# One planned kernel: load costs of the head, W^T a as columns, one operation for the weights' remainder, and scores spread by TensorE

## The chip, the cores and the metric

The kernel runs on one core of a Trainium2 chip. The metric is device time in microseconds, the median of several runs; lower is better. The engines are named as in the profile: PE is TensorE's matmul stream, PEld its weight loads, DVE is VectorE, ACT is ScalarE, POOL is GpSimd, and SP is SyncE, which issues nearly all DMAs.

## What is computed

Two graph layers on 64 graphs of 256 nodes with 256 features. The first is a gated graph network of three steps (matrix products, an aggregation over the adjacency, and a GRU cell), the second a graph attention layer; each has a layer norm and a relu ahead of it and adds its input.

```python
h = relu(layernorm(x))                      # x: (64, 256, 256)
for i in range(3):                          # gated network, A = (adj != 0)
    m = h @ weight[i]
    aggr = einsum('bst,bsd->btd', A, m)
    gi = aggr @ w_ih.T + b_ih;  gh = h @ w_hh.T + b_hh
    r = sigmoid(i_r + h_r);  z = sigmoid(i_z + h_z)
    n = tanh(i_n + r * h_n);  h = (1 - z) * n + z * h
x = x + h
h = relu(layernorm(x))                      # attention
v = h @ W.T
e = (v @ a_left)[:, :, None] + (v @ a_right)[:, None, :]
e = where(e > 0, e, 0.2 * e);  e = where(adj == 0, -1e9, e)
x = x + softmax(e) @ v
```

## The kernel before

The 64 graphs are worked on in 32 pairs. A pair is a stream of operations: layer norm and relu, turning h into columns, three gated layers, then the attention of each graph. The aggregation is done first on h, and `weight[i]` is folded into `w_ih` once in the head (the product called G, L643), so that a gate is two products with fixed matrices: `hh` with h and matrix `i` with the aggregate.

Every large product keeps more accuracy than one pass gives: an operand is split into a rounded top part in float32r and two float16 parts, and three passes are accumulated (L706 for gates, L845 for the aggregation, L1010 and L1029 for the attention). A weight matrix `m` is split by `factor` into `fac[m]` (the top), `low[m][:, 1]` (the remainder times 4096) and `low[m][:, 0]` (the top again in float16). In `factor` ScalarE writes the top (L592), VectorE writes the remainder into a float32 scratch tile (L594) and scales it into float16 (L597), and GpSimd casts the top (L599). The other splits of the head, for the operands of G, are in `three` (L626, L627, L629).

Nothing is issued in the order in which the code is written. Each operation is entered in a `Plan` with an engine, an occupancy and a latency in ns, and the tiles that it reads and writes. `Plan.run` then places the operations one by one: of those that are ready it takes the one that can start first, and among these the one with the lowest priority value, which is a due time less the length of the chain behind it and less a lead. The leads are a table `LEAD` of some 800 numbers by operation name, with the prefixes "first", "pen", "late" and "last" for pair 0 and the last three pairs:

```python
for o in self.order():
    d = deadline(o.pair) if o.due is None else o.due
    for s in o.succs:
        d = min(d, s.prio)
    o.prio = d - o.lat
for o in self.ops:
    o.prio -= o.lead
```

The order found is fixed when the kernel is built; on the chip each engine runs its own stream in that order and waits on semaphores. The planned times serve the order alone. Up to four pairs are in flight, and the 8 PSUM banks, 28 float32 tiles and the other tiles are handed out by the same plan.

Names that matter in what follows:

- The head (`setup`): `rows_of` loads weight matrices, two blocks of 128 rows (256 KB) with each DMA (L558); `load` brings x and adj of a graph, 256 KB each (L515); `bank_of` and `transposed` turn blocks by TensorE (L608, L569); "warm" runs eleven transposes of the identity (L530). `va` holds W^T a for both halves of a, spread over all partitions (L661, copied by L665).
- `dma_turn` turns a tile by the DMA's transposing copy (L738), gathers it (L743), and `join` puts it in place by ScalarE (L751). "back" turns h back into rows after a layer, by `dma_turn` where `away` holds, else by TensorE (L916; the last pair's halves L898).
- Attention: "dot" forms the two scores of each node on VectorE (L944). The right-hand scores must lie along the free axis on every partition: "line" and "right" send them to DRAM and back, broadcast (L953, L956), and for the last pair TensorE transposes them instead (L965). Then "leaky" (L970), "mask" (L973), "max" (L975), "exps" (L981, last pair L1055), "p turn", "mix", "project", "out" (L1045, L1082) and "store" (L1048, L1085). The last two pairs mix and project in plain float32 (L1018 and L1040; the last pair in halves, L1071 and L1079). `far` is true for all pairs but the last.

Of the kernel before, what the change touches and what calls it, by code (L numbers as in the profile page):

```python
# [10 lines left out]
F32 = mybir.dt.float32  # L11
# [19 lines left out]
    "A": -227000, "G": 61000, "b_nh": -3500, "b_rz": -2000, "back 0": -13500, "back 0 gather": -253500,  # L31
    "back 0 of 0": 23000, "back 0 of 1": -20500, "back 1": -55500, "back 1 gather": -20000, "back 1 of 0": 24500,
    "back 1 of 1": 49000, "back copy 1": -67500, "c0 0": -103000, "c0 1": 2000, "c0 d": -82000, "c1 0": -14500,
    "c1 1": 4000, "c1 d": 16000, "d add 0": 73500, "d add 0 of 0": -74000, "d add 0 of 1": -6000, "d add 1": -32000,
    "d add 1 of 0": -25000, "d add 1 of 1": 43500, "d mul 0": -71000, "d mul 0 of 0": 35000, "d mul 0 of 1": -14000,
    "d mul 1": 91500, "d mul 1 of 0": 46000, "d mul 1 of 1": 12000, "d sub 0": 40500, "d sub 0 of 0": 34000,
    "d sub 0 of 1": -11000, "d sub 1": 11500, "d sub 1 of 0": 22000, "d sub 1 of 1": 26000, "dot 0": 44000,
    "dot 1": 138000, "exps 0": -58500, "exps 0 0": -500, "exps 0 1": 5000, "exps 1": 137000, "exps 1 1": 46500,
    "fill": -2000, "first A": -116500, "first A16": 14000, "first back 1": 9500, "first c0 0": 12000,
    "first c0 1": 500, "first c1 1": 3000, "first d add 0": -25500, "first d add 1": 500, "first d mul 0": -22000,  # L40
    "first d mul 1": 78500, "first d sub 0": -8000, "first d sub 1": -48000, "first dot 0": -163000,
    "first dot 1": 1000, "first exps 0": -43500, "first exps 1": -15500, "first fill": 4000, "first g0 0": -42000,
    "first g0 1": 32000, "first g0 d": 38500, "first g1 0": -8000, "first g1 1": -79500, "first g1 d": 65000,
    "first h0 1": -15000, "first h1 0": 1000, "first h1 1": -32000, "first h1 d": -500, "first hi 0": 13500,
    "first hi 1": 40000, "first in 0 eps": -16000, "first in 0 pow": 55500, "first in 0 relu": 10000,
    "first in 0 shift": 32500, "first in 0 stats": 500, "first in 1 eps": -14500, "first in 1 relu": 40000,
    "first in 1 shift": -1000, "first in 1 stats": 20000, "first in hi 0": 20000, "first in hi 1": 174000,
    "first in lo 0": 80000, "first in lo 1": -16000, "first leaky 0": -23000, "first leaky 1": -122000,
    "first line 1": -1500, "first lo 0": -8000, "first lo 1": -18500, "first load": -23500, "first m0 0": 43500,
    "first m0 1": -112500, "first m0 d": 21500, "first m1 0": 16000, "first m1 1": 5000, "first m1 d": 3500,  # L50
    "first mask 0": -20000, "first mask 1": 3000, "first mid 0 eps": -111500, "first mid 0 pow": -5000,
    "first mid 0 shift": -500, "first mid 0 stats": 31000, "first mid 1 eps": 46500, "first mid 1 pow": -12000,
    "first mid 1 relu": 29500, "first mid 1 shift": 1000, "first mid 1 stats": -38000, "first mix 0": 46500,
    "first mix 1": -42000, "first nh 0 scale": 16000, "first nh 0 topF": 14000, "first nh 1 scale": 32000,
    "first ni 0 topF": -41500, "first ni 1 topF": 1000, "first out 0": 18000, "first out 1": -16000,
    "first p copy 0": 14000, "first p turn 0": -1000, "first p turn 0 gather": 26500, "first p turn 1 gather": -1000,
    "first p0 0": 18000, "first p0 1": -500, "first p0 d": -16000, "first p1 1": 12000, "first p1 d": -11000,
    "first project 0": -3000, "first prop 0": 500, "first r 0": -16500, "first r 0 topF": -16000,
    "first r 0 topT": -500, "first r 1": 90000, "first r 1 topF": 1000, "first r 1 topT": 92000,
    "first recip": -16000, "first res 0": -52000, "first res 1": -32500, "first right 0": 2000,  # L60
    "first right 1": -37500, "first store": 8000, "first tanh 0": 500, "first tanh 1": 1000, "first total": 2000,
    "first turn 0": 15500, "first turn 1": 54000, "first turn copy 0": 1000, "first turn copy 1": -8000,
    "first u 0": 8000, "first u 1": -12000, "first u add 0": -16000, "first u add 1": -97000, "first z 0": 26500,
# [135 lines left out]
    "va": 13000, "va copy": 40500, "vec": -51000, "w 0": 192500, "w copy": -77500, "w d": 84500, "w load": 2500,  # L199
    "w turn": 1500, "w up": 41000, "warm": -38000, "z 0": 34500, "z 0 of 0": -23500, "z 0 of 0 topF": -101500,  # L200
    "z 0 of 1": -31000, "z 0 of 1 topF": -260500, "z 0 topF": -647000, "z 1": 39000, "z 1 of 0": -24000,
    "z 1 of 0 topF": -69500, "z 1 of 1": -8000, "z 1 topF": -1212500,
}


# [920 lines left out]
```

## Time and profile before

| | |
|---|---|
| median of 3 runs | 1944.39 us (1941.63 to 1945.19) |
| the profiled execution's own time | 1944.63 us |
| its span in the profile | 1942.8 us |
| PE busy | 1928.9 us, 99% of the span |
| DVE, ACT busy | 1671.6 us and 1599.6 us |
| POOL busy | 228.0 us |
| granted TensorE clock, mean | 0.999 |

The span runs from the first to the last instruction. A busy PE need not be at its peak, since matmuls are pipelined, but consecutive starts in the timeline show its pace. Idle time of an engine is listed in front of the instruction that ended it, with the engine whose work released it. Lines such as L706 are lines of the kernel as printed above.

### The profile page before, as it was taken

The page shows a single profiled execution, that of the slowest core. Times are in us where ns is not written, and L with a number is a line of the kernel's source. Part 1 is how long each engine was busy: PE and PEld are TensorE (multiplying, and loading weights), DVE is VectorE, ACT ScalarE, POOL GpSimd, SP SyncE. Part 2 cuts the span into 40 slices and gives each one's busy share as a digit, 9 for nine tenths or more (in the row PEclk, how much of TensorE's full clock was granted, in tenths as well). Part 3 has the DMA queues.
Part 4 walks back from the last instruction along what each step waited for, and adds up shares of the span by engine and source line. Part 5 has one row for each costly group of instructions (what it writes and reads, how often), then busy time and mean ns, then how long its engine had stood idle before and what let it go on. Part 6 is the DMA issues. An engine that isn't in the chain of part 4 may idle for free.

```text
span 1942.8 us, 31802 instructions
## 1 busy us (share of the span) xinstructions
PE 1928.9 (99%) x10312; PEld 1223.1 (63%) x10312; DVE 1671.6 (86%) x3964; ACT 1599.6 (82%) x2799; POOL 228.0 (12%) x280
## 2 busy tenths in 40 slices
PE   8999999999999999999999999999999999999998
PEld 6656666666665666666666656666666666566677
DVE  7678889888889888898888898888988888988877
ACT  6668888888988888888889888888888888888876
POOL 4001011111011111011110111110111111110100
PEclk9999999999999999999999999999999999999999
DMA  4137676667767667866678776677765667666732
GB/s 142 33 77 147 131 144 119 119 123 139 147 117 130 120 133 131 156 110 125 119 141 138 136 120 120 124 136 153 114 130 118 139 131 146 116 125 117 125 69 72
DMA packets 734471, 239.45 MB, mean 123 GB/s; under 512 B 658256, under 2 KB 734304, under 8 KB 734304
## 3 DMA queue, kind: packets, MB, share of 16 engines
q1 hardware_dynamic: 734272, 237.41, 64.8%
q8 instruction: 81, 1.33, 0.3%
q14 instruction: 86, 0.70, 0.1%
q10 hardware_dynamic: 32, 0.01, 0.0%
HBM read 61.09 MB, written 16.84 MB: 40 GB/s over the span
## 4 chain that ended last, share of the span: by engine, by line
PE 93%; ACT 2%; DMA 2%; DVE 1%; SPq 1%; issue 0%; POOL 0%; ACTq 0%; DVEq 0%
PE bank L706 75%; PE bank L845 9%; PE bank L1029 4%; PE bank L1010 4%; DMA full<-full 2%; PE bank L643 0%; ACT full L751 0%; ACT round L674 0%; DMA full<-in_L_gnn_w_ih_dram 0%; PE bank L1018 0%; DVE half L676 0%; ACT full L874 0%; SPq L743 0%; ACT half L679 0%; PE bank L1040 0%
## 5 line engine op out<-in xcount | busy, mean ns | idle before, releaser
L706 PE MATMUL bank<-half,low_hh 128*128 128x512 f16 (+1 forms) x2352 | 613.2, 375 | 0.8 <-DVE half L676 0.8
L706 PE MATMUL bank<-half,low 128*128 128x512 f16 (+1 forms) x2352 | 612.9, 376 | 0.3 <-ACT half L679 0.2
L706 PE MATMUL bank<-round,fac_hh 128*128 128x512 f32 (+1 forms) x1176 | 433.2, 455 | 0.0
L706 PEld LDWEIGHTS <-low 128*128 128x128 f16 x2352 | 209.5, 98 | 270.9 <-issue 68.8
L706 PEld LDWEIGHTS <-low_hh 128*128 128x128 f16 x2352 | 215.4, 98 | 254.7 <-issue 47.1
L706 PE MATMUL bank<-round,fac 128*128 128x512 f32 (+1 forms) x1176 | 372.8, 411 | 0.0
L751 ACT COPY full<-full 128x1024 uint16<-128x1024 uint16 x304 | 351.8, 1174 | 20.5 <-DMA full<-full 19.6
L773 POOL TENSOR_TENSOR small<-small,nhalf 128x2 f32<-128x2 f32 x128 | 126.2, 994 | 1403.4 <-DVE small L771 1380.7
L676 DVE SCALAR_TENSOR_TENSOR half<-bank,round 128x512 f16<-128x512 f32 (+1 forms) x254 | 173.2, 684 | 107.2 <-ACT round L674 76.7
L706 PEld LDWEIGHTS bank<-round,fac_hh 128*128 128x128 f32 x1176 | 218.3, 189 | 69.0
L706 PEld LDWEIGHTS bank<-round,fac 128*128 128x128 f32 x1176 | 218.7, 188 | 57.7 <-ACT round L674 0.2
L874 ACT ACTIVATE full<-full,vec 128x512 f32<-128x512 f32 (+1 forms) x196 | 139.4, 711 | 84.7 <-DVE full L872 82.8
L676 DVE SCALAR_TENSOR_TENSOR half<-full,round 128x512 f16<-128x512 f32 (+1 forms) x254 | 170.1, 680 | 28.0 <-ACT round L674 27.4
L679 ACT ACTIVATE half<-bank 128x512 f16<-128x512 f32 (+1 forms) x254 | 154.0, 607 | 31.6 <-PE bank L1010 19.4
L674 ACT ACTIVATE round<-full 128x512 fp32r<-128x512 f32 (+1 forms) x254 | 157.5, 637 | 27.0 <-DVE full L885 26.9
L877 ACT ACTIVATE full<-bank,b_rz 128x512 f32<-128x512 f32 (+1 forms) x196 | 132.3, 675 | 48.7 <-PE bank L706 46.1
L728 ACT ACTIVATE bank<-bank,b_nh 128x512 f32<-128x512 f32 (+1 forms) x196 | 126.5, 646 | 53.8 <-PE bank L706 53.2
L864 ACT ACTIVATE full<-bank,b_rz 128x512 f32<-128x512 f32 (+1 forms) x196 | 135.1, 690 | 24.9 <-PE bank L706 24.6
L881 DVE TENSOR_TENSOR full<-full,full 128x512 f32<-128x512 f32 (+1 forms) x196 | 142.5, 727 | 12.1 <-ACT full L874 11.2
L869 DVE SCALAR_TENSOR_TENSOR full<-full,bank 128x512 f32<-128x512 f32 (+1 forms) x196 | 131.1, 670 | 18.4 <-ACT full L864 14.7
L674 ACT ACTIVATE round<-bank 128x512 fp32r<-128x512 f32 (+1 forms) x254 | 145.9, 605 | 1.2 <-PE bank L845 1.1
L682 DVE TENSOR_SCALAR half<-full 128x512 f16<-128x512 f32 (+1 forms) x254 | 124.6, 500 | 19.9 <-ACT full L751 19.8
(119 smaller groups left out, 2564.5 us busy)
## 6 DMA issues: line engine op xcount, KB each, us to landing
full<-full SPq DMA_DIRECT2D x484, 128.0 KB, 3.9
x<-in_x_dram SPq DMA_DIRECT2D x64, 256.0 KB, 3.2
adj<-in_adj_dram SPq DMA_DIRECT2D x64, 256.0 KB, 3.2
full<-in_x_dram SPq DMA_DIRECT2D x64, 256.0 KB, 3.3
full<-full SPq DMA_DIRECT2D x248, 64.0 KB, 2.2
out_dram<-full SPq DMA_DIRECT2D x62, 256.0 KB, 3.5
full<-line SPq DMA_DIRECT2D x62, 128.0 KB, 3.9
full<-full SPq DMA_TRANSPOSE x304, 3.2
```

The source lines that it names most:

```text
L674: act(f"{name} 0{of}", cut(A512 if bank else C512), lambda: nc.scalar.activation(v0.t[:, cols], v.t[:, cols], AF.Copy, scale=up), r=[(v, h ...
L676: dve_(f"{name} 1{of}", cut(V512), lambda: nc.vector.scalar_tensor_tensor(v1.t[:, cols], v.t[:, cols], up, v0.t[:, cols].bitcast(F32), op0 ...
L679: act(f"{name} d{of}", cut(A512), lambda: nc.scalar.activation(vd.t[:, cols], v.t[:, cols], AF.Copy, scale=up * unit), r=[(v, has)], w=[(v ...
L706: return [(j, lambda start, j=j, kb=kb: nc.tensor.matmul(bank.t[:, cols], fs(j, kb), s[kb][j].t[:, cols], start=start, stop=True, skip_gro ...
L728: act(name + " scale", fit(575, part), lambda: nc.scalar.activation(bank.t[:, cols], bank.t[:, cols], AF.Identity, bias=bias), r=[("b_nh", ...
L751: act(name, 1065, lambda: nc.scalar.copy(dst.t.bitcast(U16).rearrange("p (j n b) -> p j n b", j=2, b=2), src.t.bitcast(U16).rearrange(f"p ...
L845: nc.tensor.matmul(pa.t[:, ts(g, N)], b, m[:, ts(sb, N)], start=(n == 0), stop=True, skip_group_check=True)
L864: act(f"r {db}{of}", fit(575, part), lambda b=r_, k=pr, db=db, cols=cols: nc.scalar.activation(b.t[:, cols], k.t[:, cols], AF.Tanh, bias=b ...
L869: dve(f"u {db}{of}", fit(S512, part), lambda u=u, k=ph, b=r_, cols=cols: nc.vector.scalar_tensor_tensor(u.t[:, cols], b.t[:, cols], 1.0, k ...
L874: act(f"tanh {db}{of}", fit(615, part), lambda u=u, en=en, cols=cols: nc.scalar.activation(u.t[:, cols], u.t[:, cols], AF.Tanh, bias=b_i[: ...
L877: act(f"z {db}{of}", fit(575, part), lambda b=z_, k=pz, db=db, cols=cols: nc.scalar.activation(b.t[:, cols], k.t[:, cols], AF.Tanh, bias=b ...
L881: dve2(f"d sub {db}{of}", fit(V512, part), lambda u=u, d=d, cols=cols: nc.vector.tensor_sub(d.t[:, cols], d.t[:, cols], u.t[:, cols]), r=[ ...
```

## The change

In words:

- `dma_first`: loads of x, adj and the residual's x of pair 0 are planned with 1000 ns of SP and a latency of 3900 ns; `rows_of` charges 1000 ns where it charged 500. Head operations have names per matrix ("w load ih", "w 1 f0"), so that the lead table can treat them apart, and the whole table has new values (three of some 800 entries are as they were).
- `factor`: where the scale times 4096 is 1, the remainder is written at once as source minus 4096 times the top. With the new scales this holds for the twelve splits of G and for two of `w_hh` (its second half). GpSimd's cast has a region of its own, and gates and "project" name it as read.
- `va`: TensorE forms W^T a as four columns with W as the stationary operand, VectorE copies them, and four transposes of broadcast columns spread them.
- `away`: the third layer's "back" of pair 0 goes by DMA, as in later pairs.
- "dot": for the last pair the right-hand scores of both blocks come first, then the left-hand ones.
- "right": the last pair but one also spreads its right-hand scores by TensorE.

The lead table's rows for the head, old and new, with the other rows left out:

```diff
-    "va": 13000, "va copy": 40500, "vec": -51000, "w 0": 192500, "w copy": -77500, "w d": 84500, "w load": 2500,
-    "w turn": 1500, "w up": 41000, "warm": -38000, "z 0": 34500, "z 0 of 0": -23500, "z 0 of 0 topF": -101500,
...
+    "w 1 0": -227000, "w 1 1": 15000, "w 1 2": -44000, "w 1 f0": 1000, "w 1 f2": 9500, "w 1 fW": 38000,
...
+    "w load 0": 143000, "w load 1": 85500, "w load 2": -31500, "w load W": 37000, "w load full": 5000,
+    "w load hh": -8000, "w load ih": 192500, "w load x": 79000, "w turn": -151500, "w turn 2": -21500,
```

The code:

```diff
+    def dma_first(name, kb, fn, **kw):
+        plan.op(name, "SP", 1000, 3900, fn, **kw)
...
-        dma("load", 256, lambda: nc.sync.dma_start(parts(b), rows(src, g)), w=[(b, ALL)], ahead=ahead, **kw)
+        (dma if g >= G else dma_first)("load" if g >= G else f"w load {cls}", 256, lambda: nc.sync.dma_start(parts(b), rows(src, g)), w=[(b, ALL)], ahead=ahead, **kw)
...
-                plan.op("w load", "SP", 500, 3900, lambda b=b, r0=r0: nc.sync.dma_start(parts(b), view[:, r0 : r0 + 2, :]), w=[(b, ONE)])
+                plan.op(f"w load {tag}", "SP", 1000, 3900, lambda b=b, r0=r0: nc.sync.dma_start(parts(b), view[:, r0 : r0 + 2, :]), w=[(b, ONE)])
...
-            dve_("w 1", 75 + 1.04 * n, lambda: nc.vector.scalar_tensor_tensor(
-                t.t[:, :n], src(), up, top.bitcast(F32), op0=ALU.mult, op1=ALU.subtract),
-                r=[(b, ONE), (f"fac{m}", (key + (0,),))], w=[(t, ONE)])
-            dve2("w up", 75 + 0.52 * n, lambda: nc.vector.tensor_scalar(cross, t.t[:, :n], SPLIT, None, op0=ALU.mult),
-                 r=[(t, ONE)], w=[(f"fac{m}", (key + (1,),))])
-            pool("w d", 90 + 1.1 * n, lambda: nc.gpsimd.tensor_copy(rem, top.bitcast(F32)),
-                 r=[(f"fac{m}", (key + (0,),))], w=[(f"fac{m}", (key + (1,),))])
+            if up * SPLIT == 1.0:
+                dve_(f"w 1 f{m}", 75 + 1.04 * n, lambda: nc.vector.scalar_tensor_tensor(
+                    cross, top.bitcast(F32), -SPLIT, src(), op0=ALU.mult, op1=ALU.add),
+                    r=[(b, ONE), (f"fac{m}", (key + (0,),))], w=[(f"fac{m}", (key + (1,),))])
+            else:
...
+            pool(f"w d f{m}", 90 + 1.1 * n, lambda: nc.gpsimd.tensor_copy(rem, top.bitcast(F32)),
+                 r=[(f"fac{m}", (key + (0,),))], w=[(f"fac{m}", (key + (2,),))])
...
-        transposed(lambda c: whhT[c].t[:, :H], lambda c: (whhT[c], ONE), whh_n[3:], 2 * D - H, up=UP_F)
+        transposed(lambda c: whhT[c].t[:, :H], lambda c: (whhT[c], ONE), whh_n[3:], 2 * D - H, up=UP_G)
...
-            factor("hh", whhT[kb], kb, 1, bank=False)
+            factor("hh", whhT[kb], kb, 1, bank=False, up=C)
...
-                    factor(i, pg, db, half, up=1.0 / UP_H)
+                    factor(i, pg, db, half, up=C)
...
-        pl = Buf("bank")
-
-        def go():
+        pc, pl = Buf("bank"), Buf("bank")
+
+        def columns_of():
+            for db in range(DB):
+                for ob in range(DB):
+                    nc.tensor.matmul(pc.t[:, 2 * db : 2 * db + 2], parts(Wb)[:, ob, ts(db, P)], vec[:, ob : 2 * DB : DB],
+                                     start=(ob == 0), stop=(ob == DB - 1))
+
+        def spread():
             for n in range(2):
-                for ob in range(DB):
-                    c = n * DB + ob
-                    nc.tensor.matmul(pl.t[:, ts(n, D)], vec[:, c : c + 1].to_broadcast([P, P]), parts(Wb)[:, ob, :],
-                                     start=(ob == 0), stop=(ob == DB - 1))
-
-        pe("va", 4 * MM, go, r=[(Wb, ONE), ("vec", ONE)], w=[(pl, ONE)])
+                for db in range(DB):
+                    nc.tensor.transpose(pl.t[:, n * D + db * P : n * D + (db + 1) * P],
+                                        va_c[:, 2 * db + n : 2 * db + n + 1].to_broadcast([P, P]), ident)
+
+        pe("va", 4 * 110, columns_of, r=[(Wb, ONE), ("vec", ONE)], w=[(pc, ONE)])
+        dve("va column", 70, lambda: nc.vector.tensor_copy(va_c, pc.t[:, : 2 * DB]), r=[(pc, ONE)], w=[("va_c", ONE)])
+        pe("va spread", 4 * TR, spread, r=[("va_c", ONE), ("ident", ONE)], w=[(pl, ONE)])
...
-                               (f"fac{m}", tuple((kb, half, j) for kb in range(DB) for j in range(2))) for m, _ in ts_], w=[(bank, ONE)]))
+                               (f"fac{m}", tuple((kb, half, j) for kb in range(DB) for j in range(3))) for m, _ in ts_], w=[(bank, ONE)]))
...
-            away = far and p > 0
+            away = far and (p > 0 or i > 1)
...
-            for nb in range(NB):
-                for n in range(2):
+            for nb, n in [(nb, n) for nb in range(NB) for n in range(2)] if far else [(nb, n) for n in (1, 0) for nb in range(NB)]:
...
-                        r=[(hb[g], (nb,)), ("va", ONE)], w=[(sm, (c,)), (sc[g], (nb,))])
+                        r=[(hb[g], (nb,)), ("va", ONE)] + ([] if far or n == 1 else [(sm, (14, 15))]), w=[(sm, (c,)), (sc[g], (nb,))])
...
-            if p < NPAIR - 1:
+            if p < NPAIR - 2:
                 line, pR = Buf("line"), Buf("full")
```

## The prediction

> **What bounds the kernel now.** I read in this order: the page's busy table, the table of stretches, what TensorE waited for, the timeline of the head and of the tail, the chain of waits at both ends, and the queue rows.
>
> First the page's busy table, then the stretches (columns: stretch, its length, busy time of PE, PEld, DVE, ACT, POOL with counts, granted clock, DMA share, GB/s).
>
> ```profile
> PE 1928.9 (99%) x10312; PEld 1223.1 (63%) x10312; DVE 1671.6 (86%) x3964; ACT 1599.6 (82%) x2799; POOL 228.0 (12%) x280
> ```
>
> ```profile
> 0.00:10.00 10.00, 6.65 (x29) 5.62 (x29) 4.45 (x21) 3.68 (x7) 4.88 (x14) 1.00 0.80 257
> 10.00:20.00 10.00, 8.96 (x57) 6.24 (x55) 8.14 (x20) 9.18 (x25) 4.27 (x9) 1.00 0.60 182
> 20.00:30.00 10.00, 9.73 (x61) 7.24 (x61) 9.70 (x26) 9.04 (x23) 5.79 (x10) 1.00 0.12 37
> 30.00:40.00 10.00, 9.20 (x49) 5.45 (x48) 9.73 (x27) 5.19 (x11) 3.03 (x6) 1.00 0.52 114
> ...
> 1000.00:1200.00 200.00, 199.97 (x1051) 124.51 (x1050) 177.97 (x426) 166.37 (x286) 24.60 (x28) 1.00 0.73 126
> ...
> 1920.00:1943.00 23.00, 17.07 (x90) 13.91 (x88) 11.28 (x38) 9.45 (x25) 0.69 (x1) 0.91 0.15 49
> ```
>
> TensorE bounds it: 1928.9 of 1942.8 us, and 199.97 of 200 in the body. It idles 13.9 us in all: 5.5 in the first 40 us (40 less 34.54), 5.7 from 1920 on, 2.7 between. A schedule can win these, a slowed clock, and whatever TensorE work is deleted. Everything else is cover.
>
> Next, the timeline of TensorE in the head (start, length, instruction, idle before it and its releaser).
>
> ```profile
> 3.27 0.98 SPq L558 DMA_DIRECT2D full<-in_L_gnn_w_hh_dram  x2
> ...
> 5.32 0.54 SPq L558 DMA_DIRECT2D full<-in_L_gnn_w_ih_dram  x1
> ...
> 6.90 3.46 PE L608 MATMUL bank<-ident,full 128*128 128x128 f32 x15 [0.42 <-DMA full<-in_L_gnn_w_ih_dram]
> ...
> 11.24 0.77 PE L608 MATMUL bank<-ident,full 128*128 128x128 f32 x5 [0.88 <-DMA full<-in_L_gnn_w_ih_dram]
> ...
> 13.71 0.60 PE L643 MATMUL bank<-round,round 128*128 128x384 f32 x2
> ```
>
> The third w_ih load is issued at 5.32, behind x, weight 0, w_hh and adj, and lands at 11.2; the first product G (L643) starts only at 13.71. The third thing is the tail.
>
> ```profile
> 1904.22 0.95 ACT L970 ACTIVATE full<-full,small 128x256 f32<-128x256 f32 x2
> ...
> 1911.04 0.95 ACT L970 ACTIVATE full<-full,small 128x256 f32<-128x256 f32 x2
> ...
> 1918.37 2.00 PE L1018 MATMUL bank<-full,full 128*128 128x256 f32 x8 [0.64 <-ACT full L751]
> ...
> 1925.23 3.68 PE L1018 MATMUL bank<-full,full 128*128 128x256 f32 x8 [1.98 <-ACT full L751]
> ```
>
> L970 is the leaky step of the last pair but one, L1018 its two mix products. TensorE's last gate product starts at 1917.35; then it waits for the other pair's attention (0.64 and 1.98 us), and the second mix takes 3.68 us where the first took 2.00.
>
> **The change part by part.**
>
> *Order of the loads.* The planner charges a head load 1000 ns of its queue in place of 500 or 600, and the leads are per matrix. By the lead table (a larger lead goes earlier; the loads' own chains differ by some 10 us only, the leads by 40 and more) SP issues w_ih x3, weight 0, then weight 1 and x, and w_hh and weight 2 late. Between 2 and 12 us the stretches show 294, 277, 332, 368 and 360 GB/s, mean 326, so 262 KB take 0.80 us. With the first load landed at 3.5 (as now), the third w_ih lands at 5.1, not 11.2, and weight 0 at 5.9. The Trainium skill, DMA: Bandwidth & Descriptors, section "Anatomy of one DMA", fits 2.0 us + bytes/436 GB/s for a transfer issued by GpSimd: an estimate of 2.6 us for this size, whatever is ahead. By that the third w_ih would land at 7.9 now; the new order moves its issue from 5.32 to about 1.7 (0.74 and two issues of 0.47), so it would win 3.6 us on that load. The row says 5.9 us now from issue to landing and 6.1 us won. I use the row. ScalarE then needs four L626 of 0.47 and L629 (0.96 and 0.76 for pairs): from about 4.5, two and two for the first half of w_ih (1.9 us) and 1.7 for weight 0, so G could start at 8.1. Until then TensorE has 0.25 + 16 transposes of 0.115, so of the 4.1 us after the warm-up (ends 3.97) it idles 2.0, as much as it does now before 8.1 (0.42 + 1.14 + 0.42). What goes is the idle after 8.1: 0.88, about 0.2 around 13, 0.17 and 0.80, so -2.0. Ends: 0 if ScalarE (9.18 and 9.04 of 10) takes over as the limit, -4.0 if all idle after 4 goes.
>
> *Remainder of the weights in one operation.* Fourteen L597 (12 of 0.352, two near 0.4) leave VectorE: 5.0 us of the 27.6 it works from 10 to 40. The 0.55 us operation stays. This is cover for the line above (the 0.80 at 34.32 waits for VectorE), not a second gain. GpSimd's cast (0.51) now has its own key, and gates wait for it; it lies 10 us ahead of them, so 0.
>
> *W^T a as columns.* Eight L661 matmuls take 1.73 us in the chain. The new eight move two columns; no row shows that. The nearest has 128 columns: L1071, 16 in 1.78, 0.11 each, so 0.89; the lower end is the planner's 0.44. I take 0.89. The four spreading transposes: 0.11 each by L815 (8 in 0.87), 0.44. Net -0.4 (to -0.85). One small VectorE copy more (0.17 by L547); TensorE has other work between.
>
> *Back of pair 0, third layer, by DMA.* Eight L916 transposes leave TensorE, 0.11 each: -0.9, in a stretch that is 50.00 of 50 busy. In their place SP issues two transposes (1.3 each) and four gathers (0.65 each), ScalarE makes two copies of 1.16, and VectorE reads SBUF; the result comes some 8 us later (3.2 to land, 3.9 for the gather, 1.16). Pair 1's gates cover it; without that cover TensorE would stand for the difference, once. Behind these SP issues stand pair 2's loads, which have a pair's time, so 0 (upper end +0.5).
>
> *Right-hand scores of the last pair but one on TensorE.* Two DMAs per graph go (L953, L956, 3.2 and 3.9 us to land, and SP holds the second until 1905.78); four transposes come, +0.44. The dots end at 1894.8 and 1900.9, the leaky steps start 9.4 and 10.1 us later; with 0.7 for transposes and the wait they start some 9 us earlier. From leaky to mix it is 14.2 us in both graphs, so the mixes could start at about 1910 and 1916, inside the gates. A PSUM bank is held meanwhile.
>
> That does not give 9 us, because the work only changes places. Two mix and two project calls are 6.9 us at 1.73 (8 in the chain's rows). What ends the kernel then is the last pair's own path from the last gate: 25.2 us now. Without the other pair in between it would be 17.4: 7.3 to the dots (0.5 to the tanh, 0.9 for two updates, 0.5 back, 0.75 residual, 1.9 norm, 1.3 relu, the rest dots), 10.1 from there (right 0.3, leaky 0.9, mask 0.75, max 0.7, exps, turn, copy, mix, project and out 4.8, store 2.7). With all four calls ahead of the last gate, gates end at 1917.6 + 7.3 and the kernel at 1942.3: -0.5. With none ahead and none waited for, it is 20.0 (25.2 less waits of 0.64, 0.24, 1.98 and 0.30, 1.7 of a slowed clock, shown below, and 0.3 of the dots): 1918.0 + 20.0 = 1938.0, -4.8. With two ahead, 1921.5 + 18.7 (midway) = 1940.2, -2.6. The lead table does not tell which; I take the middle, -2.6.
>
> Here a rule weighs. The Trainium skill, TensorE: Matmul & The Clock Gate, section on the HAM clock gate, has the clock halve after an idle window of about 3.4 us. This trace is harsher: the wait was 1.98 us and the granted clock went to 0.64, 0.50, 0.50, 0.66 between 1925 and 1929, which cost 3.68 - 2.00 = 1.7 us. By the rule a wait that short is worth itself, by the row nearly twice that; the -2.6 leans on the row. The rule also warns of the head, should the longer gap before G cool the clock; with 0.47 busy of 2 us between 4 and 6 the trace still shows 1.00, so I put 0.
>
> *Dots of the last pair, right-hand ones first.* The spread starts two dots (0.7 us) earlier, beside the left dots; 0.3 of it lies on the path and is inside the -2.6.
>
> *All leads redrawn.* 0, from +2 to -1.5: TensorE waits 2.7 us between 40 and 1900.
>
> Sum: -2.0 - 0.4 - 0.9 - 2.6 = -5.9, against the profiled execution's 1944.63 (span 1942.80 and 1.83 around it), so 1938.7. That execution lies 0.24 above the median of the runs shown, 1944.39, so I say 1938.5.
>
> **The rivals.** *The idle only moves.* ScalarE, 91% busy from 10 to 30, holds G back as the DMA did, and the other pair's products all go ahead of the last gates. What stays is the deleted work: -0.4 - 0.9 - 0.5 = -1.8, 1942.6. For it: both engines above 90% there. Against it: 5.0 us less VectorE work, and ScalarE's idle 4.2 us at the start. Here belongs also that the change does not do what it says: orders come from planned times, and if the late mixes stay where they are, the tail gives nothing.
>
> *The body breaks.* The only one on the other side. Engines run fixed orders, and 300 leads of the repeating pair are redrawn for one plan. If one VectorE or ScalarE step lands in the wrong place, TensorE waits in each of about 30 pairs. VectorE has 11% slack (177.97 of 200), and L676 already waits 104 us for L674. At 0.20 us a pair it eats the 5.9; from 0.33 the kernel is slower by over 0.2%; at 0.5 it costs 15 us, 1953.5. Against it: 199.97 of 200 shows that such an order can be planned.
>
> *All idle goes.* Head -4.0, tail -4.8, columns -0.85, back -0.9: -10.6, 1934.
>
> **How the numbers follow.** The main case 0.52, all idle 0.12, moved idle 0.23, body 0.13. A measurement of this kernel tells about 0.2%, 3.9 us, from no change: the runs shown span 1941.6 to 1945.2. Main and best case lie beyond that on the faster side (0.64); the moved idle is inside, with 0.02 of the body (0.25); slower 0.11. The range 1934.0 to 1944.5 holds the first three with their bounds and leaves out the broken body. The likeliest case alone: 1935.5 to 1940.5.
>
> **What would show it.** w_ih issued three in a row and G's first matmul near 8 us; no L597 for fac 0 to 2; TensorE's idle in 0 to 40 near 3.5; VectorE below 9 in 20 to 40; eight fewer L916; the other pair's leaky near 1896; no clock below 1.00 after 1920. I am wrong if G starts after 12, if the clock drops in the head, if TensorE is under 199 of 200 in the body, or if the path from the last gate is still 25 us.

## The result, and the profile after

The changed kernel takes 1939.36 us (median of nine runs, 1935.76 to 1941.12) against 1944.3 for the kernel before in the same session: a ratio of 0.9975, 95% interval 0.9964 to 0.9985, or 4.9 us less. Its profiled execution took 1937.42 us with a span of 1935.6, 7.2 us less than the profiled execution before. Single executions of either kernel lie up to 4 us from their median, so the two profiles show where time went, and the medians how much.

The page's busy table:

```profile
PE 1927.1 (100%) x10312; PEld 1215.8 (63%) x10312; DVE 1647.4 (85%) x3951; ACT 1600.9 (83%) x2801; POOL 195.7 (10%) x280
```

PE busy falls by only 1.8 us, so most of the gain is idle time and slowed clock that went. The table of stretches (stretch, length, busy time of PE, PEld, DVE, ACT, POOL, granted clock, DMA share, GB/s):

```profile
0.00:10.00 10.00, 7.56 (x32) 6.14 (x33) 3.64 (x15) 5.46 (x12) 3.50 (x12) 1.00 0.78 244
10.00:20.00 10.00, 10.00 (x57) 7.25 (x57) 7.41 (x23) 8.48 (x20) 5.07 (x9) 1.00 0.74 230
20.00:30.00 10.00, 10.00 (x70) 7.54 (x69) 9.09 (x29) 8.06 (x22) 3.84 (x7) 1.00 0.01 2
30.00:40.00 10.00, 10.00 (x51) 5.93 (x49) 7.99 (x19) 7.16 (x16) 5.96 (x12) 1.00 0.55 128
1000.00:1200.00 200.00, 200.00 (x1047) 123.77 (x1045) 173.68 (x425) 167.27 (x286) 19.46 (x26) 1.00 0.72 125
1760.00:1830.00 70.00, 68.64 (x372) 42.94 (x371) 59.92 (x139) 58.64 (x99) 5.31 (x8) 1.00 0.73 122
1920.00:1935.60 15.60, 11.07 (x68) 8.97 (x66) 6.84 (x23) 6.66 (x20) 0.00 (x0) 1.00 0.20 68
```

All of the idle in the first 40 us now lies in the first ten (2.44 us; it was 5.45 over the four rows). The body stays full. One stretch is worse than before: 1.36 us of idle between 1760 and 1830, where before had none from 1700 to 1860. The timeline of the head, SP and then TensorE (start, length, instruction, idle before it and its releaser):

```profile
0.74 1.47 SPq L570 DMA_DIRECT2D full<-in_L_gnn_w_ih_dram  x3
2.25 0.47 SPq L570 DMA_DIRECT2D full<-in_L_gnn_weight_dram  x1
```

```profile
3.76 1.65 PE L626 MATMUL bank<-ident,full 128*128 128x128 f32 x6
...
6.42 2.18 PE L626 MATMUL bank<-ident,full 128*128 128x128 f32 x9 [0.39 <-DMA full<-in_L_gnn_w_ih_dram]
9.29 1.12 PE L626 MATMUL bank<-ident,full 128*128 128x128 f32 x4 [0.69 <-DMA full<-in_L_gnn_weight_dram]
10.06 0.99 PE L661 MATMUL bank<-round,round 128*128 128x384 f32 x2
10.86 2.78 PE L661 MATMUL bank<-half,half 128*128 128x384 f16 x8
```

The third load of w_ih releases TensorE at 6.42, where before it did so at 11.2. (The wait at 9.29 is for weight 1, whose turn stands ahead of G; it was issued at 3.79 and took 5.5 us.) G starts at 10.06, 3.65 us earlier than before and straight behind that turn. The timeline of ScalarE, which splits the turned blocks, shows what G would have to wait for next:

```profile
4.80 0.49 ACT L644 ACTIVATE round<-bank 128x384 fp32r<-128x384 f32 x1 [1.55 <-PE bank L626]
...
8.17 1.25 ACT L647 ACTIVATE half<-bank 128x384 f16<-128x384 f32 x3
9.28 0.69 ACT L644 ACTIVATE round<-bank 128x256 fp32r<-128x256 f32 x2
```

The top parts of weight 0 (128x256, L644) come behind all eight pieces of w_ih (128x384) and end at 9.97. G's first product needs the first of them, done at 9.70, and starts at 10.06, so ScalarE stands close behind weight 1's turn as a limit. The eight float16 products of G take 2.78 us, where before they took 1.47; more on that below. The end, ScalarE's leaky steps and then TensorE from the last gate product:

```profile
1896.46 0.84 ACT L994 ACTIVATE full<-bank,small 128x256 f32<-128x256 f32 x2 [0.40 <-PE bank L989]
...
1900.26 0.83 ACT L994 ACTIVATE full<-bank,small 128x256 f32<-128x256 f32 x2
```

```profile
1913.54 0.40 PE L731 MATMUL bank<-round,fac 128*128 128x256 f32 x2
1913.78 1.89 PE L1042 MATMUL bank<-full,full 128*128 128x256 f32 x8
...
1916.54 1.99 PE L1042 MATMUL bank<-full,full 128*128 128x256 f32 x8
1918.37 3.62 PE L1064 MATMUL bank<-wT,full 128*128 128x256 f32 x16
...
1927.68 0.93 PE L1087 MATMUL bank<-ident,full 128*128 128x128 f32 x4 [0.94 <-ACT full L1079]
```

The other pair's leaky steps (L994) come 7.8 and 10.8 us earlier than before. All four of its mix and project calls (L1042, L1064) stand behind the last gate product and start without a wait: they fill the time in which the last pair's residual, norm and dots run. The waits of 0.64 and 1.98 us and the slowed clock between them are gone. What is left is 0.94 us, behind the last pair's own exps (L1079), and 0.32 us.

To place the gain, I give each matmul of both traces its usual pace (the median distance to the next start for its shape and operands). What a stretch has beyond the sum of these is lost time: idle, a slow clock, or a matmul record missing from the trace.

| lost, us | before | after | difference |
|---|---|---|---|
| 0 to 40 | 9.03 | 7.16 | -1.9 |
| 40 to 200 | 1.21 | 0.52 | -0.7 |
| 200 to 1700 | 5.51 | 4.83 | -0.7 |
| 1700 to 1860 | 0.34 | 2.19 | +1.9 |
| 1860 to the last gate | 2.03 | 0.47 | -1.6 |
| start of the last gate product to the end (whole path) | 25.31 | 21.97 | -3.3 |
| TensorE work deleted ahead of the last gate | | | -0.8 |

They sum to -7.2 (rounded), the difference of the two spans. Against the medians' -4.9, 2.3 us of this belongs to the two executions. The rows themselves vary: in `after_again`, a second execution of the changed kernel (below), the first 40 us lose 2.0 us less than in the table, but 40 to 200 loses 0.9 more and 1700 to 1860 1.0 more, and its span is only 0.3 us shorter.

### The profile page after: what moved, and what is told of

It is laid out like the page before. It is cut to its first block, busy times and chain, and to the rows that moved or that the text cites. A ratio compares the mean times of both kernels' runs of the same rounds, so it can differ in the third digit from the quotient of the medians.

```text
span 1935.6 us, 31604 instructions
## 1 busy us (share of the span) xinstructions
PE 1927.1 (100%) x10312; PEld 1215.8 (63%) x10312; DVE 1647.4 (85%) x3951; ACT 1600.9 (83%) x2801; POOL 195.7 (10%) x280
## 4 chain that ended last, share of the span: by engine, by line
PE 95%; DMA 1%; ACT 1%; DVE 1%; SPq 1%; issue 0%; ACTq 0%
PE bank L731 76%; PE bank L870 9%; PE bank L1053 4%; PE bank L1034 4%; DMA full<-full 1%; PE bank L661 1%; SPq L768 0%; DMA full<-in_L_gnn_weight_dram 0%; ACT full L804 0%; ACT round L717 0%; PE bank L1095 0%; PE bank L1042 0%; ACT full L776 0%; DVE half L701 0%; PE bank L626 0%
## 5 line engine op out<-in xcount | busy, mean ns | idle before, releaser
L731 PE MATMUL bank<-half,low_hh 128*128 128x512 f16 (+1 forms) x2352 | 613.7, 376 | 0.0
L731 PE MATMUL bank<-half,low 128*128 128x512 f16 (+1 forms) x2352 | 611.7, 375 | 0.1
L731 PE MATMUL bank<-round,fac_hh 128*128 128x512 f32 (+1 forms) x1176 | 411.6, 437 | 0.0
L731 PE MATMUL bank<-round,fac 128*128 128x512 f32 (+1 forms) x1176 | 394.9, 425 | 0.0
L731 PEld LDWEIGHTS <-low 128*128 128x128 f16 x2352 | 216.2, 98 | 267.3 <-issue 45.4
L731 PEld LDWEIGHTS <-low_hh 128*128 128x128 f16 x2352 | 206.2, 98 | 265.3 <-issue 78.8
L731 PEld LDWEIGHTS bank<-round,fac 128*128 128x128 f32 x1176 | 218.6, 189 | 61.4
L731 PEld LDWEIGHTS bank<-round,fac_hh 128*128 128x128 f32 x1176 | 217.2, 189 | 62.7
L798 POOL TENSOR_TENSOR small<-small,nhalf 128x2 f32<-128x2 f32 x128 | 113.3, 893 | 1266.7 <-DVE small L796 1197.6
L701 DVE SCALAR_TENSOR_TENSOR half<-bank,round 128x512 f16<-128x512 f32 (+1 forms) x254 | 171.6, 683 | 50.2 <-ACT half L704 31.8
L701 DVE SCALAR_TENSOR_TENSOR half<-full,round 128x512 f16<-128x512 f32 (+1 forms) x254 | 170.3, 679 | 8.9 <-ACT round L699 6.2
L699 ACT ACTIVATE round<-bank 128x512 fp32r<-128x512 f32 (+1 forms) x254 | 152.0, 599 | 16.6 <-PE bank L870 11.5
L718 DVE SCALAR_TENSOR_TENSOR half<-full,round 128x512 f16<-128x512 f32 x184 | 125.9, 686 | 41.4 <-ACT round L717 35.6
L908 DVE SCALAR_TENSOR_TENSOR full<-full,full 128x512 f32<-128x512 f32 (+1 forms) x196 | 130.4, 676 | 33.4 <-ACT full L902 33.1
L906 DVE TENSOR_TENSOR full<-full,full 128x512 f32<-128x512 f32 (+1 forms) x196 | 132.8, 678 | 23.3 <-ACT full L899 23.0
L704 ACT ACTIVATE half<-bank 128x512 f16<-128x512 f32 (+1 forms) x254 | 142.6, 601 | 3.7 <-PE bank L870 3.1
```

Source lines behind the costliest of these rows:

```text
L699: act(f"{name} 0{of}", cut(A512 if bank else C512), lambda: nc.scalar.activation(v0.t[:, cols], v.t[:, cols], AF.Copy, scale=up), r=[(v, h ...
L701: dve_(f"{name} 1{of}", cut(V512), lambda: nc.vector.scalar_tensor_tensor(v1.t[:, cols], v.t[:, cols], up, v0.t[:, cols].bitcast(F32), op0 ...
L704: act(f"{name} d{of}", cut(A512), lambda: nc.scalar.activation(vd.t[:, cols], v.t[:, cols], AF.Copy, scale=up * unit), r=[(v, has)], w=[(v ...
L731: return [(j, lambda start, j=j, kb=kb: nc.tensor.matmul(bank.t[:, cols], fs(j, kb), s[kb][j].t[:, cols], start=start, stop=True, skip_gro ...
L906: dve2(f"d sub {db}{of}", fit(V512, part), lambda u=u, d=d, cols=cols: nc.vector.tensor_sub(d.t[:, cols], d.t[:, cols], u.t[:, cols]), r=[ ...
L908: dve2(f"d mul {db}{of}", fit(V512, part), lambda d=d, b=z_, cols=cols: nc.vector.scalar_tensor_tensor(d.t[:, cols], b.t[:, cols], 1.0, d. ...
```

## The experiments

**Loads, one step alone and the whole order undone.** `ih_early` is the kernel before with its third w_ih load issued right behind the second; nothing else moves on any engine.

```diff
-x x ih ih w0 hh hh adj adj ih ...
+x x ih ih ih w0 hh hh adj adj ...
```

> The kernel before with every engine's order as it is, except that SP issues the third w_ih load right behind the second. Theory A: it lands near 6 us in place of 11.2 and the idle 0.88 us in front of its transposes goes, while the w_hh loads land 0.8 us later; G starts 0.5 to 1.5 us earlier than 13.71 and the time falls by as much. Rival: TensorE's order holds these transposes behind those of w_hh, so nothing moves (within 0.5 us).

`old_landings` is the changed kernel with every engine's order kept, but with the loads of the head issued in the order of before.

```diff
-ih ih ih w0 x x w1 W adj adj hh hh hh w2
+x x ih ih w0 hh hh adj adj ih hh w1 w2 W
```

> The changed kernel with every engine's order as it is, except that SP issues the fourteen loads of the head in the order of the kernel before (x, two of w_ih, weight 0, two of w_hh, adj, then the third w_ih and the rest). Theory A: the third w_ih lands near 11 us in place of 6.4, G starts after 12.5 in place of 10.06, TensorE's idle time in the first 40 us grows from 2.4 to about 5, and the time is 2 to 3.5 us above the changed kernel's. Rival: ScalarE's splits or the slow clock of the head hold G back anyway, and it costs under 1 us.

The first gave 1943.45 us, 1.1 less than before, a ratio of 0.9996 (0.9987 to 1.0004): not told from none, nor from the gain of 0.5 to 1.5 us that its theory A forecast. The second gave 1942.95, 3.6 more than the changed kernel (95% interval by resampling the single times, those of `after_again` included, 2.7 to 5.2); its ratio to before is 0.9992 (0.9984 to 1.0001). The timeline of TensorE in the second:

```profile
6.01 1.85 PE L641 MATMUL bank<-ident,full 128*128 128x128 f32 x6 [2.04 <-DMA full<-in_L_gnn_w_ih_dram]
...
11.30 3.03 PE L641 MATMUL bank<-ident,full 128*128 128x128 f32 x13 [2.83 <-DMA full<-in_L_gnn_w_ih_dram]
14.63 1.01 PE L676 MATMUL bank<-round,round 128*128 128x384 f32 x2 [0.30 <-ACT round L659]
```

L641 and L676 are L626 and L661 of the changed kernel. Two waits of 2.04 and 2.83 us for w_ih come in and G goes to 14.63. In `ih_early`,

```profile
8.71 3.89 PE L623 MATMUL bank<-ident,full 128*128 128x128 f32 x16 [0.21 <-DMA full<-in_L_gnn_weight_dram]
...
14.15 0.59 PE L658 MATMUL bank<-round,round 128*128 128x384 f32 x2
```

TensorE has no wait from 8.71 on, and G still starts at 14.15 (13.71 before): its fixed order has 28 transposes ahead of G, and until 12.99 they run at half clock. So the head's gain needs the new load order. That it also needs the engine orders planned around it is likely but not shown, since `ih_early` moves one load alone.

**The remainder in two operations again.** `two_ops` is the changed kernel with the remainder written in two VectorE operations through a scratch tile, inside one planned operation of the same planned time, so that the order stays.

```diff
-nc.vector.scalar_tensor_tensor(cross, top, -SPLIT, src(), op0=ALU.mult, op1=ALU.add)
+nc.vector.scalar_tensor_tensor(t.t[:, :n], src(), up, top, op0=ALU.mult, op1=ALU.subtract)
+nc.vector.tensor_scalar(cross, t.t[:, :n], SPLIT, None, op0=ALU.mult)
```

> The changed kernel with the weights' remainder in two VectorE operations again (fourteen times); the planned costs and the order of all engines stay. The prediction (one operation is cover only): VectorE works 5 us more in the head, TensorE's idle time in the first 40 us grows by 0 to 0.8 us, and the time stays within 1 us of the changed kernel's. Rival: VectorE bounds the head, and the 5 us appear as 2 to 5 us of time.

It gave 1941.26 us, 1.9 more (by the same resampling 1.0 to 3.4; ratio to before 0.9981, 0.9975 to 0.9988). The stretches of its head, and TensorE's waits (waited for: us in total, times, longest):

```profile
20.00:30.00 10.00, 9.39 (x60) 6.51 (x59) 9.90 (x31) 6.77 (x19) 3.81 (x7) 1.00 0.01 2
30.00:40.00 10.00, 9.36 (x48) 5.36 (x47) 9.14 (x22) 5.62 (x13) 5.23 (x10) 1.00 0.36 79
```

```profile
PE bank L731 <- DVE full L607: 0.6, 1, 0.6
PE bank L870 <- DVE half L718: 0.6, 2, 0.3
PE bank L581 <- DVE full L612: 0.4, 1, 0.4
```

VectorE is at 9.90 of 10, TensorE loses 0.6 us in each ten, and each wait names VectorE. Its lost time from 14 to 40 us is 1.95, against 0.1 to 0.3 in the changed kernel's executions. So the operation is not cover alone, and the 1 us that was expected at most is missed: it carries about as much as the term of the load order was given.

**Fillers against a slow clock.** `fill_one` and `fill_two` are the changed kernel with four, and with seven, idle transposes put into its head, meant for the gaps in which TensorE waits for loads; `after_again` is the changed kernel beside them.

```diff
+for _ in range(4):
+    nc.tensor.transpose(pt.t[:, ts(3, P)], ident, ident)
```

> The changed kernel once more, as the base for the three kernels run beside it on the same chip. Ratio to the kernel before 0.9964 to 0.9985 as before. If TensorE's half clock in the head ends at a free-running moment, the pace of its transposes shows it ending at another time than 13.86 us.

> The changed kernel with four more transposes of the identity (no use is made of them) on TensorE in the gap of 0.9 us before weight 0 is turned; nothing else differs. Theory C (the half clock costs time in the head: matmuls of 384 columns follow each other by 320 ns until 13.86 us and by 163 after[...]): the pace doubles near 10.4, the first products G take 1.5 us less, and the time falls by 1 to 1.7 us below the changed kernel's. Rival D (the splits on ScalarE and VectorE bound the head there, so faster products only wait): under 0.4 us.

> As the kernel with one gap filled, and three more transposes of the identity in the gap of 0.65 us before the third w_ih load's blocks are turned. Theory C: the pace may double near 7.0 already; transposes then take 0.11 in place of 0.21, but weight 0 lands at 9.3 whatever the clock, so it gains at most 0.5 us over the kernel with one gap filled. Rival D: no difference to the changed kernel.

Measured: 1939.40, 1939.40 and 1938.89 us, ratios to before 0.9973, 0.9974 and 0.9971. In time there is nothing to tell, and the first filler missed its gap. The load that lands last ahead of G is weight 1's, not weight 0's. The four transposes ahead of weight 0's turn run without a break in `fill_one`, and the wait comes behind them:

```profile
6.83 0.60 PE L626 MATMUL bank<-ident 128*128 128x128 f32 x4
7.26 0.60 PE L626 MATMUL bank<-ident,full 128*128 128x128 f32 x4
9.20 0.66 PE L626 MATMUL bank<-ident,full 128*128 128x128 f32 x4 [1.34 <-DMA full<-in_L_gnn_weight_dram]
9.61 0.60 PE L661 MATMUL bank<-round,round 128*128 128x384 f32 x2
```

In the traces the clock differs, but not through the fillers: it was full at 4.20 us in `fill_one` and at 5.85 in `fill_two`, before their first idle transposes ran (6.83 and 5.89), and at 4.91 in `after_again`, which has none. The same lines of `after_again` are

```profile
8.57 0.66 PE L626 MATMUL bank<-ident,full 128*128 128x128 f32 x4 [1.62 <-DMA full<-in_L_gnn_weight_dram]
8.98 0.67 PE L661 MATMUL bank<-round,round 128*128 128x384 f32 x2
9.49 2.14 PE L661 MATMUL bank<-half,half 128*128 128x384 f16 x8
```

with four transposes in 0.66 us instead of 1.12, from the same code. Whether fillers make the full clock likelier stays open; with intervals of 2 us either way, nothing of 0.5 us can be told. In these executions a head that runs sooner does not bring its whole gain to the end, either: between 1700 and 1860 TensorE waits 2.6 us for VectorE's splits (L701) in `fill_one` and 2.2 in `after_again`, where it waits 1.36 in the first execution.

**The score spread.** `undo_right` takes it out of the changed kernel: the last pair but one sends its right-hand scores through DRAM again.

```diff
-            if p < NPAIR - 2:
+            if p < NPAIR - 1:
```

> The changed kernel, but the last pair but one spreads its right-hand scores by the two DMAs again; the plan is made anew and differs only near the end. Theory A (the change gains in three places: the order of the head's loads, deleted TensorE work, and the tail through these scores): that pair's leaky steps move about 8 to 9 us later again, the way from the start of the last gate product to the end grows from the 22.1 us of the changed kernel to 24 to 26, and the time is 2.5 to 4 us above the changed kernel's, so a ratio to the kernel before of 0.9985 to 1.000. Theory B (the redrawn lead table does it, the scores hardly matter): under 1 us above the changed kernel.

`right_alone` puts it into the kernel before, with the opposite edit and the old leads.

> The kernel before with one part of the change: the last pair but one spreads its right-hand scores by TensorE. Theory A: its leaky steps start near 1896 and 1902 in place of 1904 and 1911, the wait of 1.98 us in front of the second mix and the clock drop behind it go, and the time falls by 2 to 3.5 us (ratio 0.998 to 0.999). Theory B: without the new leads nothing is gained, within 1 us.

`undo_right` gave 1941.43 us, 2.1 more than the changed kernel (by the same resampling 0.6 to 3.7; ratio to before 0.9982, 0.9976 to 0.9989). The time lies a little below what theory A named, and the path is not as it said. ScalarE's leaky steps and TensorE's wait behind the last gate are

```profile
1906.54 0.94 ACT L994 ACTIVATE full<-full,small 128x256 f32<-128x256 f32 x2
...
1919.54 0.84 PE L923 MATMUL bank<-ident,full 128*128 128x128 f32 x4 [1.81 <-DVE full L910]
```

The leaky steps come 10.1 and 11.3 us later again, but the path from the last gate grows only to 22.9 us, 1.0 more and not 2 to 4; another 1.1 us is lost between 1860 and the last gate. So with the scores through DRAM 2.4 of the path's 3.3 us are still won.

`right_alone` gave 1951.65, 7 us *more* than before (1.0038, 1.0025 to 1.0051). The same edit has both signs. In the second kernel, ScalarE, then TensorE, then the stretches:

```profile
1926.46 0.59 ACT L1036 COPY full<-bank 128x512 f32<-128x512 f32 x1 [2.75 <-PE bank L1018]
1926.94 2.07 ACT L779 ACTIVATE full<-full,small 128x256 f32<-128x256 f32 x4
```

```profile
1931.09 0.82 PE L965 MATMUL bank<-ident,small 128*128 128x128 f32 x2 [2.00 <-DVE full L944]
...
1934.96 1.18 PE L1063 MATMUL bank<-ident,full 128*128 128x128 f32 x4 [2.02 <-ACT full L1055]
```

```profile
1920.00:1930.00 10.00, 8.39 (x41) 6.58 (x39) 7.69 (x30) 4.79 (x9) 1.34 (x2) 1.00 0.08 26
1930.00:1940.00 10.00, 6.63 (x26) 5.09 (x27) 5.63 (x23) 5.51 (x17) 0.00 (x0) 0.56 0.08 26
```

In the fixed order, the copy of the other pair's second mix (L1036) stands on ScalarE ahead of the last pair's relu (L779). The copy waits 2.75 us for its product, the relu of the last two graphs starts only at 1926.94 (1918.59 in the kernel before), the dots and the right-hand scores come behind it, TensorE waits 2.00 and 2.02 us, and the clock falls to 0.56. From the last gate product it is 30.0 us, where it was 25.3.

**The lead table.** `old_leads` is the changed kernel with the old leads for all pairs but the first; `new_leads` the kernel before with the new ones for the same operations. In both, the head and pair 0 keep their own.

```diff
-LEAD[name] of the one table, for every name outside the head and "first ..."
+LEAD[name] of the other table
```

> The changed kernel with the lead table of the kernel before for every operation of the pairs but the first (the head and pair 0 keep their new leads). Theory A, the table and the edits are one piece, an order drawn for one set of operations fits no other: the head's gain stays (about -2), the deleted TensorE work stays (-0.8), and the end goes as in the kernel before with the score spread alone, which lost 7 us: 1944.3 - 2.8 + 7 = 1948.5, between 1945 and 1952; the path from the last gate's start 28 us or more, or new waits of TensorE between 40 and 1860 us. Theory B, the edits carry the gain and the leads are worth nothing on their own (the prediction's 0): 1939 to 1941, path from the last gate 22.

> The kernel before with the new lead table for every operation of the pairs but the first (the head and pair 0 keep their old leads). Theory A, table and edits are one piece: at or above the kernel before, 1944 to 1950, with new waits of TensorE in the body or a path from the last gate of 25 us or more. Theory B, the leads are worth nothing: 1944.3, path 25.3. Theory C, the new table carries the tail's gain by itself, as the changed kernel with the old score path (tail 22.9 us) suggests: -2.4 at the tail, 1942, path about 23.

`undo_back` is the changed kernel with pair 0's third "back" on TensorE again.

```diff
-            away = far and (p > 0 or i > 1)
+            away = far and p > 0
```

> The changed kernel with pair 0's third-layer back on TensorE again, eight transposes instead of two DMA turns; all else as changed, the order planned anew. By the prediction's step: +0.9 us, 1940.3, no other difference. Theory A (an order fits only the operations it was drawn with; here the operation undone lies at the start of the body): more than +0.9, 1941 to 1945, with new waits of TensorE between 40 and 1860 us.

The three gave 1997.53 us (ratio 1.0278, 1.0264 to 1.0292), 1959.24 (1.0078, 1.0065 to 1.0091) and 1957.13 (1.0066, 1.0053 to 1.0079), beside 1943.52 for before: 54, 16 and 14 us slower. All three went past every number given for them, the first by far. Its waits of TensorE, and its body:

```profile
PE bank L1391 <- DVE half L1361: 15.4, 11, 3.9
PE bank L1694 <- DVE half L1361: 13.6, 12, 1.7
```

```profile
200.00:1700.00 1500.00, 1467.63 (x7706) 908.26 (x7705) 1260.49 (x3003) 1234.07 (x2128) 151.06 (x196) 1.00 0.71 127
```

(Its table is printed one entry a line, so L1391 is the gate product L731, L1694 the mix L1034, L1361 the remainder of a split, L701.) VectorE and ScalarE are busy for less time than in the changed kernel's body, 1260 and 1234 us of 1500 against 1300 and 1269, and TensorE still waits for VectorE's splits 23 times. The engines are not short of time; the splits come in the wrong place of the order. The path from the last gate is 22.8 us, not the 28 expected, though only because one mix and one project of the other pair (3.5 us) now stand ahead of the last gate. Against the changed kernel's profile some 40 us are lost between 200 and 1700, 7 ahead of that, and about 13 from 1860 to the end.

The body of `new_leads` is sound (5.9 us lost from 200 to 1700, before 5.5). It loses 12.4 us in the first 40 (before 9.0), 8.7 from 40 to 200 (1.2) and 5.3 from 1700 to 1860 (0.3), among it a mix that waits 5.4 us for VectorE's split near the start of the body, and a project that waits 2.4 us late. `undo_back` puts back eight transposes of 0.11 us near the start, but TensorE's and ScalarE's rows near the end are

```profile
1933.12 3.60 PE L1064 MATMUL bank<-wT,full 128*128 128x256 f32 x8 [2.49 <-ACT full L1060]
...
1940.88 2.17 PE L1087 MATMUL bank<-ident,full 128*128 128x128 f32 x8 [3.65 <-ACT full L1079]
```

```profile
1931.51 1.09 ACT L804 ACTIVATE full<-full,small 128x256 f32<-128x256 f32 x2 [2.92 <-DMA out_dram<-full]
1932.51 0.56 ACT L1060 COPY full<-bank 128x512 f32<-128x512 f32 x1
```

The plan is greedy, so one operation changed in pair 0 can shift every later choice, and 1900 us further on the relu stands ahead of the mix copy and waits 2.92 us for a store. Of the 17.8 us by which it is slower than the changed kernel, 10.5 lie on the path from the last gate (32.4 us), and none of it says what the eight transposes cost.

## Why the prediction was right, and where its steps were off

The predicted time, 1938.5 us, lies 0.9 us from the median and the case came out as the main one. Its working did less well than its total: terms that were off stand on both sides, so part of the closeness is luck.

- *Order of the loads, -2.0.* The head (to 40 us) gained 1.9 by the two traces, 3.9 with `after_again` for after. SP's order was as derived. The landings were near it in one execution and 1.3 us late in the other: the third w_ih 5.25 and 6.35 (5.1 predicted), weight 0 6.25 and 7.15 (5.9), each the issue time plus the time to landing, in `after_again` and in the first execution. G came at 8.98 and 10.06 (8.1), and two things in the step failed. It left out a wait: weight 1's turn stands ahead of G, its load lands at 8.57 and 9.29, and G starts within 0.1 us of that turn's last transpose in both executions. And it miscounted ScalarE, the next limit: the step had it split half of w_ih ahead of weight 0, the order has all eight pieces, so the first top is done at 8.88 and 9.70. In `fill_one` both tops of weight 0 are done by 9.32, and G at 9.61 still waits for the turn. The rule weighed there, 2.6 us a load whatever is ahead, fits the first two loads (2.8 and 3.0 us) and none of the rest (4.6 to 6.0 in the first execution). `old_landings` puts the order at 3.6 us, near the step's end of -4.0.
- *The clock in the head, "I put 0".* This was wrong, and the row for it stood among those shown: 15 transposes in 3.46 us are 0.23 each (they start 0.213 apart), while the step counted with 0.115. The granted-clock column says 1.00 there, but that record begins only when the full clock is first granted: at 10.40 us in the kernel before, at 13.86 in the changed kernel's execution. Up to then consecutive float16 products of G start 320 ns apart, from then on 163. So the changed kernel won 3.65 us on G's start and gave about 1.5 of it back over G's first ten products (3.12 us to the start of the next, before 1.62), in this execution.
- *Remainder in one operation, 0 beyond cover.* Mis-sized: 1.9 us by `two_ops`. The step saw 0.80 us of wait for VectorE and held it inside the load order's gain. With loads early, VectorE would be the next limit at 9.90 of 10.
- *W^T a as columns, -0.4, and back of pair 0, -0.9.* The new matmuls start 0.11 us apart, as chosen, and not 0.055 as planned. With the late scores' four transposes (+0.44) the steps delete 0.86 us; by paces it is 0.8. What the DMA back costs besides could not be measured alone.
- *Late scores, -2.6.* In part right: the leaky steps came at 1896.5 (1896 predicted), no clock below 1.00 until the last instruction, and the path from the last gate was 22.0 us. The case was the one called "none ahead and none waited for", for which the step said 20.0 and -4.8. It got -3.3: two waits of 0.94 and 0.32 us remain, where the step had none. `undo_right` puts the edit at 2.1, but only 1.0 of that lies on the path. The other 2.4 us of the path's gain, which the step laid to the scores, came without them; whether the new leads or the order of the last pair's dots brought them was not tried.
- *All leads redrawn, 0 from +2 to -1.5.* By the first execution the term fits: +1.9 from 1700 to 1860, -0.7 twice before. With `after_again` for after it is +2.8, +0.2 and -0.8, a little over the +2 named. (TensorE's 2.7 us of idle, which the step put between 40 and 1900, lie between 40 and 1920; to 1900 they are 2.1.) The new cost is a split that VectorE does late; in the first execution and in `after_again` the row is

```profile
1778.54 1.05 PE L1053 MATMUL bank<-low_W,half 128*128 128x256 f16 x8 [0.68 <-DVE half L701]
1778.37 1.05 PE L1053 MATMUL bank<-low_W,half 128*128 128x256 f16 x8 [1.60 <-DVE half L701]
```

  As a thought it was the weak step. It priced the redraw beside the edits, as if these could be had without it. `old_leads`, `right_alone` and `undo_back` show that they cannot: with leads drawn for another set of operations, one is 54, one 7 and one 14 us slower. The rival of a broken body had the right mechanism, VectorE's step in the wrong place; at 45 us lost between 200 and 1700, about 25 pairs, it runs at 1.8 us a pair, beyond the 0.5 priced. It did not occur in the changed kernel, whose table was drawn for its edits.

The terms depend on each other and need not add: the undo runs in the head and at the score spread give 3.6 + 1.9 + 2.1 = 7.6 us, more than the whole gain of 4.9, though by the noise of single executions (4.5 to 12.0 for the sum) not surely more. What the new table loses near 1780 and 1820 is part of the difference; how the rest splits stays open. One rival was not run: the kernel before with a table drawn anew for its own operations. Without it, how much of the 4.9 us a better table alone could bring is not known.

The rival in which the idle only moves did not come, but its reading was off: it had both engines above 90% from 10 to 30 us, and VectorE stood at 89 (8.14 and 9.70 of 10).

A rule stands behind the head's clock. The Trainium skill, TensorE: Matmul & The Clock Gate, Part 1 on the HAM clock gate, has TensorE start at half clock and reach the full one after about 3.4 us of sustained work. By that, with TensorE busy from 1.36 to 6.02 us without a break and for 7.56 us of the first ten, the full clock would be there before 10 us. Here it came at 13.86 in one execution and at 4.91 in another of the same kernel, so in this head the rule gives the size of the slowdown (320 against 163 ns) but not its end.

## What to carry to other kernels

In a kernel whose order is fixed by a plan, an edit has no price of its own: cost it together with the order that was drawn for it, and when one is undone or tried alone, look first at how the order changed, far from the edit too. Check the pace of an operation in a long timeline row (length by count; a short row holds the whole length of its last one) against its pace elsewhere before trusting a clock column that reads 1.00. Check in the trace that a filler stands in the gap it was meant for. When the wait at the head of a chain goes, ask which engine stands at nine tenths in the same stretch: the relief that looked like cover is then part of the gain.

## What the hardware showed that was not expected

- Full clock after the start is granted at different times in executions of much the same head: 4.91, 4.20, 5.85 and 13.86 us in four of the changed kernel and its fillers, 10.40 in the kernel before. In `two_ops` it came at 4.92 and left again from 8.34 to 11.75, and in `undo_right` it came at 5.00 and left from 8.41 to 15.23. Between `after_again` and the first execution of the changed kernel the lost time in the first 40 us differs by 2.0 us, but the spans by 0.3.
- In `right_alone` the clock fell to half at 1931.3, just behind a wait of 2.00 us, and stayed there to 1941.5, with another wait of 2.02 in between. In the kernel before, a wait of 1.98 was followed by 3.4 us at half clock (1925.28 to 1928.69), which cost 1.7 us of time.
- Matmuls of two columns with a 128 x 128 stationary operand in float32 (L678) start 0.11 us apart, as far apart as those of 128 columns: below that size fewer columns bring nothing here. Each has its own block to load (eight loads in 1.03 us), so which of the two sets the pace is open.
- A load of 256 KB took 2.8 to 6.0 us from issue to landing in the same head; in the first execution the first two of w_ih took 2.8 and 3.0, the third 4.6.
